# Two graph-attention layers on one core: dense products as four 128x32 column tiles, score products as eight 32x64 tiles

## The chip, the core and the metric

The kernel runs on one core of a Trainium2 chip. The core has a tensor engine (TensorE, PE in the profile, with its weight loads as a row of their own, PEld), a vector engine (DVE), a scalar engine (ACT), GpSimd (POOL) and a queue engine (SP) that issues transfers. The metric is device time in microseconds of one execution; several executions of a kernel are timed and the median is taken.

TensorE multiplies a stationary operand, which is loaded first (a weight load), with a moving operand that streams past it. The stationary operand of a matmul is given as `lhsT` (rows are the contraction, columns become output partitions), the moving one as `rhs`. A matmul may use the whole 128x128 array or a tile of it: a shape such as 128x32 in this text is rows by columns of the stationary operand. Where an operand lies decides the tile: rows by the partitions of the inputs, columns by the partitions of the output.

## The reference

32 graphs of 512 nodes with 256 features each, and an integer adjacency matrix per graph. Two attention layers of 8 heads of 32 follow each other, the first with a feed-forward block of 1024 hidden units, each with residuals and layer norms. Everything is float32.

```python
# layer 0, x: (32, 512, 256), adj: (32, 512, 512)
allowed = (adj > 0) | (swapaxes(adj, 1, 2) > 0) | eye
q, k, v = heads(split(x @ Wqkv.T + bqkv))            # 8 heads of 32
s = where(allowed, (q / sqrt(32)) @ k.T, -inf)
h = layernorm(x + concat(softmax(s) @ v) @ Wo.T + bo)
h = layernorm(h + relu(h @ W1.T + b1) @ W2.T + b2)
x = layernorm(x + h)
# layer 1: attention with the mask adj != 0 and weights of its own
x = layernorm(x + attention(x, adj) @ Wo.T + bo)
```

## The kernel before

The work on one graph is cut into small methods of a class `Graph`, each of which issues a few instructions: a burst on TensorE, an activation, a step of a norm, a transfer. The order is written out by hand. `opening` starts the first graphs, `period` is repeated for the graphs in the middle with up to five graphs in flight (`a` to `e`, each in another stage), and `closing` ends the last ones. Each engine runs its instructions in the order in which these three functions issue them. The trace shows about 95 us for one period.

N is 512 nodes (4 blocks of 128), D is 256 features (2 blocks of 128), a block of 128 features holds 4 heads of 32. Activations are kept with features on the partitions for TensorE (`xT`, `qT`, `kT`, `cT`) and with nodes on the partitions for the norms. The bursts on TensorE, by method:

- `transpose` (L303): four 128x128 transpositions by the identity, into one PSUM tile.
- `query_key` (L332): for one block of 128 output features, two matmuls over the 2 input blocks, moving 512 or 256 nodes. ACT adds the bias (L335).
- `value` (L315): 2 blocks of nodes, each two matmuls moving 256 features. ACT copies (L322).
- `scores` (L345): for one half of the heads and one block of 128 keys, four matmuls, one per head: stationary 32 rows (the head's features) by 128 keys, moving 32 x 512 queries, each into a PSUM bank of its own. ACT then takes the exponential of the whole 128x2048 tile (L349), and DVE multiplies with the mask (`masked`, L354).
- `product` (L362): four matmuls, one per head: stationary 128 keys by 32 features, moving 128 x 512 of the exponentials, into 32 output partitions each; over 4 blocks of keys it accumulates. ACT copies the sum (L372).
- `sums` (L402): the same shape with a stationary block of ones, for the denominators, after DVE and transfers have added up the exponentials (`fold`, L381; `pair`, L377).
- `project` (L461): 2 blocks of nodes, each two matmuls moving 256.
- `hidden` (L481): two blocks of hidden units, each two matmuls moving 256 nodes; ACT applies the ReLU (L489).
- `mlp` (L502): one block of nodes, eight matmuls over the hidden blocks moving 256, one accumulation.

PSUM is shared out so: `ps_s` has one buffer of four banks for scores, `ps_a` one bank for `product`, `ps_d` three single banks for everything else. So a score burst waits until the exponential of the one before has been read, and a dense burst until the one that used its bank three before has been read.

In the kernel before, `query_key`, `value`, `project`, `hidden` and `mlp` use a 128x128 stationary block, as `transpose` does. `scores` uses 32x128 tiles, `product` and `sums` 128x32 tiles.

Of the kernel before, what the change touches and what calls it, by code (L numbers as in the profile page):

```python
# [27 lines left out]
def kernel(ctx: ExitStack, tc: tile.TileContext, t: dict, out: bass.AP):  # L28
# [12 lines left out]
    nc = tc.nc  # L41
    x, adj = t["x"], t["adj"]
    B, N, D = x.shape
    P = 128
    NQ = N // P
    ND = D // P
    HD = D // HEADS
    HPC = P // HD
    DFF = t["L0_gnn_W1"].shape[1]
    NF = DFF // P  # L50
# [36 lines left out]
    def column(name, start=0, size=D):  # L87
# [6 lines left out]
    proj = [  # L94
        (
            [wqkv[:, :, i * D : (i + 1) * D] for i in range(3)],
            column("L0_gnn_bqkv", 0),
            column("L0_gnn_bqkv", D),
            column("L0_gnn_bqkv", 2 * D),
        )  # L100
    ]
    wo = [weight("L0_gnn_Wo")]
    bo = [spread("L0_gnn_bo")]
    w1, b1 = weight("L0_gnn_W1"), column("L0_gnn_b1", 0, DFF)
    w2, b2 = weight("L0_gnn_W2"), spread("L0_gnn_b2")
# [44 lines left out]
    def plain(pools: ExitStack):  # L150
# [8 lines left out]
        def value_bias(layer):  # L159
# [6 lines left out]
            nc.vector.tensor_tensor(bov[layer], ps, bo[layer], ALU.add)  # L166

        def add_row(dst, row):
            nc.gpsimd.dma_start(out=dst, in_=row[:, None, :].to_broadcast([P, NQ, D]), accum_op=ALU.add)
# [7 lines left out]
        class Graph:  # L177
# [129 lines left out]

            def value(self, layer, h):
                if h == 0 and layer != 0:
                    self.tile("v", [NQ, D])  # L310
                ps = ps_d.tile([P, 2, D], F32, tag="d", name=f"psV_{self.b}_{h}")
                for j in range(2):
                    at = slice((2 * h + j) * P, (2 * h + j + 1) * P)
                    for i in range(ND):
                        nc.tensor.matmul(  # L315
                            ps[:, j, :],
                            self.xT[:, i, at],
                            proj[layer][0][2][:, i, :],
                            start=(i == 0),
                            stop=(i == ND - 1),  # L320
                        )
                nc.scalar.copy(self.v[:, 2 * h : 2 * h + 2, :], ps)  # L322

            def query_key(self, layer, which, c, h=None):

                tag = ("qT", "kT")[which]
                dst = getattr(self, tag) if c or h or (which and layer == 0) else self.tile(tag, [ND, N])
                w, bias = proj[layer][0][which], proj[layer][1 + which]
                at = slice(0, N) if h is None else slice(h * 2 * P, (h + 1) * 2 * P)
                ps = ps_d.tile([P, at.stop - at.start], F32, tag="d", name=f"psQK_{self.b}_{which}_{c}_{h}")  # L330
                for i in range(ND):
                    nc.tensor.matmul(  # L332
                        ps, w[:, i, c * P : (c + 1) * P], self.xT[:, i, at], start=(i == 0), stop=(i == ND - 1)
                    )
                nc.scalar.activation(dst[:, c, at], ps, AF.Identity, bias=bias[:, c : c + 1])  # L335


            def scores(self, layer, k):
                if k == 0:
                    self.layer, self.p, self.acc = layer, {}, {}  # L340
                hg, kc = divmod(k, NQ)
                s = ps_s.tile([P, HPC, N], F32, tag="s", name=f"psS_{self.b}_{k}")
                for j in range(HPC):
                    at = slice(j * HD, (j + 1) * HD)
                    nc.tensor.matmul(  # L345
                        s[:, j, :], self.kT[at, hg, kc * P : (kc + 1) * P], self.qT[at, hg, :], start=True, stop=True
                    )
                p = work.tile([P, HPC, N], F32, tag="p", name=f"p_{self.b}_{k}", bufs=8)
                nc.scalar.activation(p, s, AF.Exp, scale=SCALE)  # L349
                self.p[k] = p  # L350
# [101 lines left out]

            def project(self, layer, h):

                if h == 0:
                    self.y, self.po = {}, {}
                ps = ps_d.tile([P, 2, D], F32, tag="d", name=f"psO_{self.b}_{layer}_{h}")
                for j in range(2):
                    at = slice((2 * h + j) * P, (2 * h + j + 1) * P)
                    for k in range(ND):  # L460
                        nc.tensor.matmul(  # L461
                            ps[:, j, :], self.cT[:, k, at], wo[layer][:, k, :], start=(k == 0), stop=(k == ND - 1)
                        )
                self.po[h] = ps
# [6 lines left out]

            def hidden(self, h, f):

                if f == 0:
                    self.hT = getattr(self, "hT", {})
                    self.hT[h] = work.tile([P, NF, 2 * P], F32, tag="hT", name=f"hT_{self.b}_{h}", bufs=1)
                ps = ps_d.tile([P, 2, 2 * P], F32, tag="d", name=f"psH_{self.b}_{h}_{f}")
                for j in range(2):
                    at = slice((f + j) * P, (f + j + 1) * P)
                    for c in range(ND):  # L480
                        nc.tensor.matmul(  # L481
                            ps[:, j, :],
                            w1[:, c, at],
                            self.xT[:, c, h * 2 * P : (h + 1) * 2 * P],
                            start=(c == 0),
                            stop=(c == ND - 1),
                        )
                for j in range(2):
                    nc.scalar.activation(self.hT[h][:, f + j, :], ps[:, j, :], AF.Relu, bias=b1[:, f + j : f + j + 1])  # L489
# [7 lines left out]

            def mlp(self, i):
                h, j = divmod(i, 2)
                ps = ps_d.tile([P, D], F32, tag="d", name=f"psF_{self.b}_{i}")  # L500
                for f in range(NF):
                    nc.tensor.matmul(  # L502
                        ps, self.hT[h][:, f, j * P : (j + 1) * P], w2[:, f, :], start=(f == 0), stop=(f == NF - 1)
                    )
                self.pf[i] = ps
# [36 lines left out]
        def period(a, b, c, d, e):  # L542
# [36 lines left out]
            a.out1(0)  # L579
            a.project(1, 1)  # L580
            b.norm2(2)
# [10 lines left out]
            b.transpose(b.x2, 1)  # L592
            b.query_key(1, 1, 0, 0)
            c.product(4)
# [66 lines left out]
            a.store()  # L661
            d.value(0, 0)
            b.scores(1, 6)
# [16 lines left out]
            c.transpose(c.x1, 1)  # L680
            d.query_key(0, 1, 0)
            d.value(0, 1)
            d.query_key(0, 0, 0)
            d.query_key(0, 0, 1)
            c.mlp(0)
            d.query_key(0, 1, 1)
            c.residual1()
            c.mlp(1)
            b.product(3)
# [18 lines left out]
        def opening(a, b, c, d):  # L708
# [8 lines left out]
            a.join(0, 1)  # L717
            a.query_key(0, 0, 0)
            a.query_key(0, 1, 0)
            a.value(0, 0)  # L720

# [67 lines left out]
            b.scores(0, 3)  # L789
            b.query_key(0, 0, 1)  # L790
            a.project(0, 1)
            b.entries()
# [28 lines left out]
            a.transpose(a.x1, 1)  # L821
            a.mlp(0)
            a.mlp(1)
            a.residual1()
# [25 lines left out]
            a.transpose(a.x2, 0)  # L850
            a.mlp(3)
            a.out2(3)
            b.masked(0, 6)
            a.root(2, 3, 4)
            a.mlp(2)
            a.out2(2)
# [24 lines left out]
            c.join(0, 0)  # L881
            a.query_key(1, 0, 0, 0)
            a.query_key(1, 0, 0, 1)
            a.query_key(1, 1, 0, 1)
            c.value(0, 0)

# [38 lines left out]
            b.transpose(b.x1, 0)  # L925
            c.query_key(0, 1, 0)
            c.masks()
# [15 lines left out]
            b.transpose(b.x1, 1)  # L943
            b.mlp(0)
            b.mlp(1)
            b.residual1()
# [16 lines left out]
        def closing(a, b, c):  # L963
# [8 lines left out]
            c.scores(0, 1)  # L972
            b.hidden(1, 6)
            b.transpose(b.x2, 0)
# [42 lines left out]
            b.transpose(b.x2, 1)  # L1017
            b.query_key(1, 0, 0, 0)
            b.query_key(1, 1, 0, 0)
            c.pair(4)  # L1020
            b.query_key(1, 0, 0, 1)
            c.masked(0, 7)
# [4 lines left out]
            c.fold(3, 3, 4)  # L1027
            b.query_key(1, 1, 1)

# [29 lines left out]
            c.norm1(0)  # L1059
            c.project(0, 1)  # L1060
            c.transpose(c.x1, 0)
# [12 lines left out]
            c.transpose(c.x1, 1)  # L1074
            c.mlp(1)
            c.mlp(0)
            b.masked(1, 6)
# [5 lines left out]
            c.out2(1)  # L1083
            c.hidden(1, 0)
            b.masked(1, 2)
# [3 lines left out]
            c.norm2(1)  # L1089
            c.hidden(1, 4)  # L1090
            c.hidden(1, 6)
            c.hidden(1, 2)
            b.product(0)
# [30 lines left out]
            b.fold(3, 6, 7)  # L1124
            c.query_key(1, 1, 0, 0)
            c.query_key(1, 0, 0, 1)
            c.query_key(1, 1, 0, 1)

# [288 lines left out]
```

## Time and profile before

| | |
|---|---|
| median of 3 runs | 3074.48 us (3072.88 to 3076.89) |
| span of the profiled execution | 3072.4 us |
| DVE busy, mean of one mask or fold (128x2048) | 2648.1 us, 2.28 us |
| ACT busy, one exponential (128x2048) | 1707.3 us, 1.88 us |
| POOL busy | 1039.0 us |
| share of the DMA engines by queue | 51.2% + 16.1% + 0.3% + 0.1% |
| HBM traffic | 40 GB/s over the span |

TensorE's groups, which the profile adds up by line:

| line | burst | instructions | busy us | mean ns |
|---|---|---|---|---|
| L345 | scores | 4096 | 583.9 | 640 |
| L362 | product | 4096 | 492.7 | 598 |
| L502 | mlp | 2048 | 468.5 | 382 |
| L481 | hidden | 2048 | 467.3 | 384 |
| L461 | project | 1024 | 241.0 | 383 |
| L402 | sums | 1072 | 139.8 | 598 |
| L303 | transpose | 520 | 87.3 | 289 |

A matmul's duration in the trace runs from its start to a modelled end and overlaps the next one's, so the mean of one is longer than the time it takes up in a stream; the busy time of a group is the time covered by at least one of its instructions. Each float32 matmul of the program appears as two matmul instructions and two weight loads; a transposition as one of each.

### The profile page before, as it was taken

What the parts mean: (1) busy time and instruction counts of PE and PEld (TensorE: products, weight loads), DVE (VectorE), ACT (ScalarE), POOL (GpSimd) and SP (SyncE); (2) the same over time, 40 slices, a digit from 0 to 9 for tenths busy, and PEclk for the clock granted to TensorE, in tenths of its full rate; (3) what the DMA queues carried; (4) which work ended last, traced back from release to release, by engine and by line L of the source; (5) the groups of instructions that cost most, each with busy time, mean ns of one, the idle gap of its engine ahead of it and who ended that gap; (6) DMA issues with size and microseconds to landing.
All of it is one profiled execution on the core that took longest, in us unless ns stands there. A gap on an engine that the chain in (4) does not pass through costs nothing. (4 is left out here: it accounts for less than half of the span.)

```text
span 3072.4 us, 44237 instructions
## 1 busy us (share of the span) xinstructions
PE 3049.0 (99%) x17218; PEld 1728.9 (56%) x17218; DVE 2648.1 (86%) x3458; ACT 1707.3 (56%) x1983; POOL 1039.0 (34%) x1254
## 2 busy tenths in 40 slices
PE   8999999999999999999999999999999999999998
PEld 4555655556555555555555555655556555555564
DVE  6798889888889888898888988889888889888887
ACT  5455565555556555565556655565555556555554
POOL 1333333433334332343323333333433334332332
PEclk9999999999999999999999999999999999999999
DMA  9876677666767666676666766667766767666543
GB/s 207 155 141 129 116 141 145 140 123 126 136 138 148 121 131 124 138 154 122 133 124 136 148 134 131 114 141 145 139 124 126 136 137 148 120 131 124 117 83 70
DMA packets 341064, 406.54 MB, mean 132 GB/s; under 512 B 149616, under 2 KB 315632, under 8 KB 316144
## 3 DMA queue, kind: packets, MB, share of 16 engines
q0 software_dynamic: 95824, 282.09, 51.2%
q1 hardware_dynamic: 245024, 121.56, 16.1%
q8 instruction: 137, 2.24, 0.3%
q14 instruction: 79, 0.65, 0.1%
HBM read 89.01 MB, written 33.55 MB: 40 GB/s over the span
## 5 line engine op out<-in xcount | busy, mean ns | idle before, releaser
L349 ACT ACTIVATE p<-psS 128x2048 f32<-128x2048 f32 x512 | 962.2, 1879 | 657.1 <-PE psS L345 655.4
L354 DVE TENSOR_TENSOR p<-p,m 128x2048 f32<-128x2048 f32 x512 | 1155.4, 2279 | 8.4 <-ACT p L349 8.2
L436 POOL TENSOR_SCALAR rs<-mv 128x2 f32<-128x2 f32 (+1 forms) x320 | 326.3, 1020 | 940.6 <-DVE mv L431 939.7
L345 PE MATMUL psS<-qT,kT 32*128 32x512 f32 x4096 | 583.9, 640 | 2.8 <-ACT p L349 1.3
L362 PE MATMUL psA<-p,v 128*32 128x512 f32 x4096 | 492.7, 598 | 0.9 <-ACT cT L372 0.7
L502 PE MATMUL psF<-w_L_gnn_W,hT 128*128 128x256 f32 x2048 | 468.5, 382 | 0.0
L481 PE MATMUL psH<-xT,w_L_gnn_W 128*128 128x256 f32 x2048 | 467.3, 384 | 0.7 <-DMA w_L_gnn_W<-in_L_gnn_W_dram 0.7
L502 PEld LDWEIGHTS psF<-w_L_gnn_W,hT 128*128 128x128 f32 x2048 | 383.8, 190 | 123.0 <-issue 76.4
L481 PEld LDWEIGHTS psH<-xT,w_L_gnn_W 128*128 128x128 f32 x2048 | 381.4, 190 | 120.3 <-issue 47.9
L381 DVE TENSOR_TENSOR p<-p,p 128x2048 f32<-128x2048 f32 x189 | 429.5, 2286 | 6.4 <-DMA p<-p 4.7
L345 PEld LDWEIGHTS psS<-qT,kT 32*128 32x128 f32 x4096 | 159.9, 182 | 300.5 <-issue 117.2
L437 POOL TENSOR_TENSOR rs<-rs,neg_half 128x2 f32<-128x2 f32 (+1 forms) x320 | 299.6, 936 | 26.8
L362 PEld LDWEIGHTS psA<-p,v 128*32 128x32 f32 x4096 | 109.9, 109 | 315.3 <-issue 234.5
L489 ACT ACTIVATE hT<-psH,c_L_gnn_b 128x256 f32<-128x256 f32 x512 | 215.2, 472 | 120.6 <-PE psH L481 117.3
L417 POOL TENSOR_TENSOR total<-total,sT 128x16 f32<-128x16 f32 x128 | 28.4, 222 | 732.0 <-DVE sT L414 732.0
L461 PE MATMUL psO<-w_L_gnn_Wo,cT 128*128 128x256 f32 x1024 | 241.0, 383 | 0.9 <-DVE cT L421 0.9
L332 PE MATMUL psQK_None<-xT,w_L_gnn_Wqkv 128*128 128x512 f32 x512 | 238.4, 598 | 2.4 <-DMA w_L_gnn_Wqkv<-in_L_gnn_Wqkv_dram 2.4
L372 ACT COPY cT<-psA 128x512 f32<-128x512 f32 x128 | 75.0, 586 | 280.7 <-PE psA L362 280.7
L377 POOL DMA_DIRECT2D p<-p x189 | 188.2, 996 | 117.8 <-PE psA L362 108.7
L449 DVE TENSOR_TENSOR y<-psF,x 128x256 f32<-128x256 f32 x128 | 53.9, 421 | 200.1 <-PE psF L502 197.6
L461 PEld LDWEIGHTS psO<-w_L_gnn_Wo,cT 128*128 128x128 f32 x1024 | 189.3, 190 | 52.0 <-DVE cT L421 23.0
L430 DVE BATCH_NORM_STATS2 st<-y 128x6 f32<-128x256 f32 x384 | 164.3, 428 | 13.1
(68 smaller groups left out, 2930.8 us busy)
## 6 DMA issues: line engine op xcount, KB each, us to landing
p<-p POOLq DMA_DIRECT2D x189, 1024.0 KB, 7.7
x<-in_x_dram SPq DMA_DIRECT2D x64, 512.0 KB, 5.1
x<-bov POOLq DMA_DIRECT2D x64, 512.0 KB, 9.2
code<-in_adj_dram POOLq DMA_DIRECT2D x32, 512.0 KB, 6.6
m<-code SPq DMA_DIRECT2D x32, 512.0 KB, 5.6
x<-s_L_gnn_ln_b POOLq DMA_DIRECT2D x32, 512.0 KB, 10.4
x<-s_L_gnn_b POOLq DMA_DIRECT2D x32, 512.0 KB, 5.4
out_dram<-x SPq DMA_DIRECT2D x32, 512.0 KB, 9.1
```

The costliest lines, as they stand in the source:

```text
L332: nc.tensor.matmul(ps, w[:, i, c * P : (c + 1) * P], self.xT[:, i, at], start=(i == 0), stop=(i == ND - 1))
L345: nc.tensor.matmul(s[:, j, :], self.kT[at, hg, kc * P : (kc + 1) * P], self.qT[at, hg, :], start=True, stop=True)
L349: nc.scalar.activation(p, s, AF.Exp, scale=SCALE)
L354: nc.vector.tensor_tensor(p, p, m[:, k % NQ, None, :].to_broadcast([P, HPC, N]), ALU.mult)
L362: nc.tensor.matmul(self.acc[hg][j * HD : (j + 1) * HD, :], self.v[:, kc, h * HD : (h + 1) * HD], self.p[k][:, j, :], start=(kc == 0), stop ...
L381: nc.vector.tensor_tensor(self.p[dst], self.p[a], self.p[b], ALU.add)
L436: nc.gpsimd.tensor_scalar(rs, self.mv[n][:, a:b, 1:2], EPS, None, ALU.add)
L437: nc.gpsimd.tensor_tensor(rs, rs, neg_half[:, a:b, None], ALU.pow)
L461: nc.tensor.matmul(ps[:, j, :], self.cT[:, k, at], wo[layer][:, k, :], start=(k == 0), stop=(k == ND - 1))
L481: nc.tensor.matmul(ps[:, j, :], w1[:, c, at], self.xT[:, c, h * 2 * P : (h + 1) * 2 * P], start=(c == 0), stop=(c == ND - 1),)
L489: nc.scalar.activation(self.hT[h][:, f + j, :], ps[:, j, :], AF.Relu, bias=b1[:, f + j : f + j + 1])
L502: nc.tensor.matmul(ps, self.hT[h][:, f, j * P : (j + 1) * P], w2[:, f, :], start=(f == 0), stop=(f == NF - 1))
```

## The change

A new helper `dense` issues one product either as one 128x128 matmul (`wide`) or as four matmuls over 32 columns of the stationary operand each, into 32 output partitions each, with the same moving operand. The five dense methods call it and take an argument `wide`, which is false unless a call in `opening`, `period` or `closing` sets it. It is set at 10 calls of `period` and at further calls of the other two functions, next to `transpose` in the order. `value_bias` and `transpose` stay as they are. `scores` issues two matmuls per head instead of one, for 64 keys each. The order of all bursts and the work of all other engines stay as they were.

```diff
+        def dense(out, lhsT, rhs, start, stop, wide):
+            for at in (slice(0, P),) if wide else [slice(j * HD, (j + 1) * HD) for j in range(HPC)]:
+                nc.tensor.matmul(out[at], lhsT[:, at], rhs, start=start, stop=stop)
...
-            def value(self, layer, h):
+            def value(self, layer, h, wide=False):
...
                     for i in range(ND):
-                        nc.tensor.matmul(
-                            ps[:, j, :],
-                            self.xT[:, i, at],
-                            proj[layer][0][2][:, i, :],
-                            start=(i == 0),
-                            stop=(i == ND - 1),
-                        )
+                        dense(ps[:, j, :], self.xT[:, i, at], proj[layer][0][2][:, i, :], i == 0, i == ND - 1, wide)
...
             def scores(self, layer, k):
...
                     at = slice(j * HD, (j + 1) * HD)
-                    nc.tensor.matmul(
-                        s[:, j, :], self.kT[at, hg, kc * P : (kc + 1) * P], self.qT[at, hg, :], start=True, stop=True
-                    )
+                    for half in range(2):
+                        key = kc * P + half * P // 2
+                        nc.tensor.matmul(
+                            s[half * P // 2 : (half + 1) * P // 2, j, :],
+                            self.kT[at, hg, key : key + P // 2],
+                            self.qT[at, hg, :],
+                            start=True,
+                            stop=True,
+                        )
...
         def period(a, b, c, d, e):
...
-            a.project(1, 1)
+            a.project(1, 1, wide=True)
...
-            b.query_key(1, 1, 0, 0)
+            b.query_key(1, 1, 0, 0, wide=True)
...
-            d.value(0, 0)
+            d.value(0, 0, wide=True)
...
-            d.query_key(0, 1, 0)
-            d.value(0, 1)
-            d.query_key(0, 0, 0)
-            d.query_key(0, 0, 1)
-            c.mlp(0)
-            d.query_key(0, 1, 1)
+            d.query_key(0, 1, 0, wide=True)
+            d.value(0, 1, wide=True)
+            d.query_key(0, 0, 0, wide=True)
+            d.query_key(0, 0, 1, wide=True)
+            c.mlp(0, wide=True)
+            d.query_key(0, 1, 1, wide=True)
             c.residual1()
-            c.mlp(1)
+            c.mlp(1, wide=True)
```

`query_key`, `project`, `hidden` and `mlp` change as `value` does.

## The prediction

> **What bounds the kernel now.** I read the page's busy shares first, then the waits of TensorE (PE), then PE's timeline over some 30 us of a middle period, then the weight loads (PEld).
>
> ```profile
> PE 3049.0 (99%) x17218; PEld 1728.9 (56%) x17218; DVE 2648.1 (86%) x3458; ACT 1707.3 (56%) x1983; POOL 1039.0 (34%) x1254
> ...
> PEclk9999999999999999999999999999999999999999
> ```
>
> ```profile
> PE psT L303 <- DMA x<-in_x_dram: 4.7, 1, 4.7
> PE psQK_None L332 <- DMA w_L_gnn_Wqkv<-in_L_gnn_Wqkv_dram: 2.4, 1, 2.4
> PE psS L345 <- ACT p L349: 1.3, 1, 1.3
> ```
>
> PE is never idle after the opening: 7.1 us of waits there, about 5 us in all the rest, and the full clock throughout. The chain that ended last is only the tail behind the last matmul, so the span is PE's own sequence of bursts. What counts is the time from the start of one burst to the start of the next; a burst's printed length is modelled and overlaps its successor.
>
> ```profile
> 1502.99 1.14 PE L345 MATMUL psS<-qT,kT 32*128 32x512 f32 x8
> 1504.06 3.72 PE L502 MATMUL psF<-w_L_gnn_W,hT 128*128 128x256 f32 x16
> 1507.71 1.06 PE L402 MATMUL psR<-p,ones 128*32 128x512 f32 x8
> 1508.60 1.04 PE L362 MATMUL psA<-p,v 128*32 128x512 f32 x8
> 1509.57 1.14 PE L345 MATMUL psS<-qT,kT 32*128 32x512 f32 x8
> 1510.64 1.07 PE L362 MATMUL psA<-p,v 128*32 128x512 f32 x8
> 1511.63 3.72 PE L502 MATMUL psF<-w_L_gnn_W,hT 128*128 128x256 f32 x16
> ...
> 1520.40 1.14 PE L345 MATMUL psS<-qT,kT 32*128 32x512 f32 x8
> 1521.47 2.78 PE L362 MATMUL psA<-p,v 128*32 128x512 f32 x24
> 1524.18 1.14 PE L345 MATMUL psS<-qT,kT 32*128 32x512 f32 x8
> ...
> 1529.74 1.03 PE L332 MATMUL psQK<-xT,w_L_gnn_Wk 128*128 128x256 f32 x4
> 1530.60 1.03 PE L332 MATMUL psQK<-xT,w_L_gnn_Wq 128*128 128x256 f32 x4
> ```
>
> Columns: start in us, length, engine, line, then stationary shape (rows*columns) and moving shape. Every fp32 product is two instructions (two passes). Three things are to be seen.
>
> First, the streaming price. Four instructions of 256 columns take 0.86 us (1529.74 to 1530.60): 0.215 each, and the single records of such a burst are 0.216 apart. In the 24-instruction product run, four column tiles run side by side: 2.71 us against 0.99 for 8 instructions, so 1.72 us for four more rounds of four, 0.430 a round of 512 columns. A wide 512-column instruction is 0.429 after its predecessor. So four 128x32 tiles together stream as fast as one 128x128 tile; nothing is gained or lost there.
>
> Second, a change of tile shape costs time. Scores take 1.07 us (1502.99 to 1504.06) for 2 rounds, 0.853 at the pure rate: 0.217 lost. A product alone takes 0.99 (1510.64 to 1511.63): 0.137 lost. A wide run of 16 takes 3.65 (1504.06 to 1507.71) against 16 x 0.216 = 3.45: 0.20 lost. Between sums and product (1507.71 to 1508.60), same shape, 0.89: nearly nothing lost.
>
> Third, what the loss is made of:
>
> ```profile
> L345 PEld LDWEIGHTS psS<-qT,kT 32*128 32x128 f32 x4096 | 159.9, 182 | 300.5 <-issue 117.2
> L362 PEld LDWEIGHTS psA<-p,v 128*32 128x32 f32 x4096 | 109.9, 109 | 315.3 <-issue 234.5
> L502 PEld LDWEIGHTS psF<-w_L_gnn_W,hT 128*128 128x128 f32 x2048 | 383.8, 190 | 123.0 <-issue 76.4
> ...
> 1508.17 0.13 PEld L362 LDWEIGHTS psA<-p,v 128*32 128x32 f32 x4 [0.30 <-issue]
> ```
>
> A load of 128 columns takes 190 ns, of 32 columns 109: 0.84 ns a column, so 107 ns against 27 for the columns themselves. Four loads cover 0.13 us at 0.109 each: tiles start 7 ns apart, 20 ns for four. After the last matmul's stream ends, the next shape's first load comes 91 to 95 ns later in the records (the array empties). So wide 94 + 107 = 0.20, product 94 + 27 + 20 = 0.14, scores 91 + 107 + 20 = 0.218: all three measured losses.
>
> **The change, part by part.** I counted runs of one tile shape in the order of PE's instructions. Before: 512 score runs, 420 wide, 260 column; 1191 changes of shape. After, with bursts in the same order: 512, 131, 450; 1092 changes.
>
> Check of the sum: 512 x 0.217 + 420 x 0.20 + 260 x 0.137 = 230.7 us lost to changes. Streaming: 6664 wide passes of 256 x 0.216, 768 of 512 x 0.429, 520 transpositions x 0.109, 1024 score rounds x 0.427, 1292 column rounds x 0.429 = 2817. Together 3048 of the span of 3072.4; the opening (first matmul at 4.7, the weight's wait, slower first matmuls) and the tail behind the last projection hold the rest. The profiled execution lies 2 us below the median of the runs, 3074.5, so I take savings from the median.
>
> Dense products narrow (L163's stays wide): 289 wide runs fewer x 0.20 = -57.8; 190 column runs more x 0.137 = +26.0. Net -31.8 us. The 4964 wide passes that become rounds of four keep 0.216 or 0.429 each.
>
> Scores as 32x64: no row shows this shape. By the load's columns it saves 64 x 0.84 = 54 ns; with eight tiles 7 ns apart the last starts 47 ns behind the first, not 20: +27. Net -27 ns x 512 = -13.8 us. Bounds: as cheap as the product's 0.137, -41 us; load no shorter and the eight starts paid, +27 ns, +13.8 us. I take -13.8, since load and spacing both follow the rows.
>
> PE's instructions grow from 34,436 to 72,412, all loads and matmuls. A narrow round of 256 columns needs eight in 216 ns, 27 ns each. The longest sustained pace shown is lower, 16 in 0.43 us, but one place shows what PE's sequencer can do: while scores waited at 73.45 us, two semaphore instructions ran at 73.29 (51 ns) and 73.415, with the eight instructions of a transposition passed between, 74 ns: 9 ns each. Hidden, then, while the array streams. Their fetch queue (137 packets, 2.24 MB) about doubles; at 256 instructions a packet, one must come every 6.9 us inside a narrow run, against 18.8 at the closest now; a packet takes about 1 us.
>
> The Trainium skill speaks against this part: "TensorE: Matmul & The Clock Gate", section "Wait — 56ns, not 53.3ns?", says that without hardware decode the sequencer spends about 62 ns per matmul, which binds when the array work per matmul is shorter. Narrow rounds of 256 have 54 ns per matmul; by that rule 4 x 62 = 248 ns a round, 32 more in 4680 rounds, an estimated +150 us. The 9 ns of the trace contradict it.
>
> Waits: 187 more of PE's waits are on PE itself, each for a burst at least 1.7 us of matmul time back; queued behind them are only PE's own next bursts, so nothing. ACT, DVE, POOL and SP keep their instructions and order. PE comes earlier by 1.4 us in each period of 95.0 us. Scores wait for the exp of the burst before (one psS buffer): exp at 1518.22 takes 1.88, the next scores start at 1520.40, 0.30 spare; between those two bursts all stays wide, so only 0.027 goes. The tightest repeated wait is the row sums' on DVE's fold, 0.2 us spare in 27 periods. PE gains some 0.35 us over the bursts that feed that fold, so about 0.15 us x 27 = 4 us comes back as waiting. Bounds: none, if DVE moves along (14% idle); (1.4 - 0.2) x 30 = 36 us, if DVE doesn't move at all.
>
> **Sum.** -31.8 - 13.8 + 4 = -41.6 us: 3074.5 - 41.6 = 3033 us.
>
> **The rivals.** *A narrow round isn't free* (slower). Its place is every narrow round of 256 columns: loads of 109 ns, four together 0.13 us, must fit beside 0.213 instead of 0.427 us of stream, and eight instructions must arrive in that time. It decides from 41.6 / 4964 = 8.4 ns a round. If the 28 ns of a load that show at a change of shape showed in every round, 4964 x 0.028 = +139: 3172 us. For it: no row has column tiles with 256 columns. Against: 0.13 fits in 0.213, and wide loads of 190 ns fit there already.
>
> *The gain is eaten by waits*: with the 36 us above and scores without gain, -31.8 + 36 = +4, up to 3078; with half of it, 3060. For it: DVE is 86% busy and mask, fold and norm stand in one fixed order. Against: PE waits hardly ever today, and half the waits that I could place have 1.8 us to spare.
>
> *Score halves don't run side by side* (the tiling doesn't do what it says): both halves of a 32-row strip stream the same qT; if one waits for the other, +0.853 us x 512 = +437, 3470 us. Against: the products' four column tiles stream through the same 128 rows together. The same page of the skill, section "Measured speedup vs the span model", gives 10.6 times for sixteen 32x32 tiles; no run here shows that.
>
> **How the numbers follow.** Forecast 0.80, narrow rounds dear 0.10, eaten 0.06, halves in turn 0.04. The forecast's own range: -31.8 - 41 = -73 (3002) to -31.8 + 13.8 + 11 (a third of the 36) = -7 (3067). Most of the eaten case lies above; dear rounds and serial halves are left out. Under 0.2% (6 us) a measurement of this kernel can't tell from no change. Faster 0.82 (the forecast and a little of the eaten case), same 0.04, slower 0.14 (both dear cases).
>
> **What would show it.** PE stays near 99%. Scores start to next start 1.04 us (1.07 before); 0.98 or 1.10 would be the bounds. A narrow mlp of 32 matmuls (x64) 16 x 0.216 plus at most 0.14. No gap between narrow hidden and product. PE's waits for DVE grow by about 4 us. It is wrong if rounds of four start over 0.224 us apart, if score records of one strip start 0.43 us apart, or if PE waits add 20 us or more.

## The result and the profile after

| | before | after |
|---|---|---|
| median of the timed runs, taken side by side | 3074.28 us (3072.88 to 3078.45, 12 runs) | 3074.61 us (3071.69 to 3078.51, 12 runs) |
| ratio, 95% interval | 1 | 1.0001 (0.9993 to 1.0009) |
| span of the profiled execution | 3072.4 us | 3073.1 us |
| one period in the middle, median from start to start | 94.79 us | 94.68 us |

The change moves nothing that can be measured; the forecast was 3033 us. The period is read from the trace's records, as the distance between the first score bursts of successive graphs.

The page of the changed kernel, its busy shares and the chain that ended last, by engine:

```profile
PE 3019.5 (98%) x36206; PEld 1393.8 (45%) x36206; DVE 2648.4 (86%) x3458; ACT 1702.8 (55%) x1983; POOL 1044.9 (34%) x1254
...
DVE 49%; PE 35%; issue 8%; DMA 4%; POOL 4%; ACT 0%; SPq 0%; DVEq 0%; POOLq 0%; ACTq 0%
```

PE is busy 29.5 us less than before in a span that is as long. And the chain, which was only the tail behind the last matmul, now runs through the whole span, half of it on DVE. PE's waits after (engine, tile and line, what it waited for; us in total, times, longest):

```profile
PE psT L308 <- DVE x L448: 21.2, 34, 0.7
PE psR L405 <- DVE p L384: 6.1, 6, 2.4
...
PE psS L344 <- ACT p L352: 2.1, 9, 0.6
```

The first of these was 0.9 us, 2 times, before, and the second wasn't in the list. The first is the transposition of x1, which needs the first norm's output from DVE. Busy times of PE in the first half of the steady stretch (from and to, length, PE busy with its instructions, PEld, DVE, ACT, POOL, clock, DMA share, GB/s), before and then after:

```profile
260.00:1530.00 1270.00, 1269.85 (x7194) 721.47 (x7187) 1111.39 (x1455) 713.03 (x827) 445.79 (x530) 1.00 0.69 134
```

```profile
260.00:1530.00 1270.00, 1257.75 (x15240) 579.27 (x15236) 1111.21 (x1456) 710.08 (x826) 451.01 (x530) 1.00 0.69 134
```

DVE does the same work in the same stretch; PE's idle time went from 0.15 to 12.25 us.

The prices of the bursts themselves came out as forecast. PE's timeline after:

```profile
1504.28 1.11 PE L344 MATMUL psS<-qT,kT 32*64 32x512 f32 x16
1505.32 3.66 PE L171 MATMUL psF<-w_L_gnn_W,hT 128*32 128x256 f32 x64
...
1512.89 3.64 PE L171 MATMUL psF<-w_L_gnn_W,hT 128*32 128x256 f32 x64
1516.34 1.91 PE L171 MATMUL psO<-w_L_gnn_Wo,cT 128*32 128x256 f32 x32
```

Scores take 1.04 us from start to start (1.07 before), and a narrow mlp of 64 instructions ahead of a burst of the same shape 3.45 us, 16 rounds of 0.216.

Now the place of the wait. Before, PE and then DVE:

```profile
1556.20 0.66 PE L303 MATMUL psT<-ident,x 128*128 128x128 f32 x4
1556.69 1.89 PE L315 MATMUL psV<-w_L_gnn_Wqkv,xT 128*128 128x256 f32 x8
```

```profile
1555.77 0.48 DVE L445 SCALAR_TENSOR_TENSOR x<-cent,rs,s_L_gnn_ln_b 128x256 f32<-128x256 f32 x1
```

After, PE and then DVE:

```profile
1556.81 0.33 PE L308 MATMUL psT<-ident,x 128*128 128x128 f32 x1
1557.85 0.55 PE L308 MATMUL psT<-ident,x 128*128 128x128 f32 x3 [0.71 <-DVE x L448]
```

```profile
1557.31 0.48 DVE L448 SCALAR_TENSOR_TENSOR x<-cent,rs,s_L_gnn_ln_b 128x256 f32<-128x256 f32 x1
```

The burst transposes two blocks of x1. Its first instruction needs the first block, the second one the second block, whose norm is this DVE instruction. After, the second starts 1.04 us behind the first instead of 0.11: PE stands 0.93 us **inside** the burst. Before, the burst already started at 1556.20, ahead of the end of that norm at 1555.77 + 0.48 = 1556.25; the second load starts at 1556.31 in the records. So the norm came just in time, with nothing to spare. In most of the kernel's other transpositions, which nothing holds up, the second load starts 0.056 to 0.061 us behind the first, here 0.113: PE already waited for the norm by some 0.05 us, and no wait was listed.

Why doesn't DVE move along? All of its gaps between 1535 and 1600 us before, and the first three of them after (in brackets the gap and what ended it):

```profile
1554.73 0.48 DVE L445 SCALAR_TENSOR_TENSOR x<-cent,rs,s_L_gnn_ln_b 128x256 f32<-128x256 f32 x1 [0.92 <-POOL rs L437]
1578.79 0.42 DVE L449 TENSOR_TENSOR y<-psF,x 128x256 f32<-128x256 f32 x1 [2.40 <-PE psF L502]
1583.96 0.42 DVE L449 TENSOR_TENSOR y<-psF,x 128x256 f32<-128x256 f32 x1 [4.07 <-PE psF L502]
1586.34 0.48 DVE L445 SCALAR_TENSOR_TENSOR z<-cent,rs,x 128x256 f32<-128x256 f32 x1 [0.91 <-POOL rs L437]
1590.21 0.73 DVE L518 TENSOR_SCALAR x<-z,mv,rs 128x256 f32<-128x256 f32 x2 [1.13 <-POOL rs L437]
```

```profile
1556.27 0.48 DVE L448 SCALAR_TENSOR_TENSOR x<-cent,rs,s_L_gnn_ln_b 128x256 f32<-128x256 f32 x1 [0.92 <-POOL rs L440]
1580.22 0.42 DVE L452 TENSOR_TENSOR y<-psF,x 128x256 f32<-128x256 f32 x1 [2.28 <-PE psF L171]
1585.39 0.42 DVE L452 TENSOR_TENSOR y<-psF,x 128x256 f32<-128x256 f32 x1 [4.07 <-PE psF L171]
```

DVE's idle 14%, some 13 us a period, isn't slack that can be spent anywhere. Half of it is two waits for the mlp products (`out2`), 2.40 and 4.07 us, which end 22 and 28 us after the transposition; the other gaps are latencies of about 1 us inside DVE's own norms, where POOL works out `rs`. From the second `y` of one period to the norm of the next, DVE's work is a chain with nothing but such latencies in it. It starts with these lines, before and after, one period ahead of those shown above:

```profile
1489.17 0.42 DVE L449 TENSOR_TENSOR y<-psF,x 128x256 f32<-128x256 f32 x1 [4.07 <-PE psF L502]
```

```profile
1490.63 0.42 DVE L452 TENSOR_TENSOR y<-psF,x 128x256 f32<-128x256 f32 x1 [4.07 <-PE psF L171]
```

It ends with the norm at 1556.25 and 1557.79: 67.1 and 67.2 us. Then PE goes from the second transposition to the end of the second mlp product: 27.65 us before (1556.31 to 1583.96), 27.54 after (1557.85 to 1585.39). With some 0.05 us from the norm's end to the load that it releases, this **loop through both engines** takes 94.79 us before and 94.76 after, the length of just these periods (most of those after have 94.67). Any path from one event to the same event of the next period adds up to that; what makes this one a bound is that no step of it has time to spare. The chain that ended last shows it after (start, length, what):

```profile
1548.49 4.48 DVE p L357 x2
1555.52 0.73 POOL rs L440
1556.27 0.49 DVE x L448
1556.79 0.50 DVE cent L447
1557.31 0.50 DVE x L448
1557.85 0.55 PE psT L308 x3
1558.40 1.73 PE psV L171 x8
...
1581.89 3.45 PE psF L171 x16
```

Before, PE's own sequence took 94.78 us, the period of the two runs below that relieve the loop in that kernel (`e4_before_mlp_early`, `e6_before_no_mask`): two bounds within some 0.01 us of each other. The change shortened one of them by 1.4 us. In the other, it touches two score bursts (2 x 0.027) and one run of `hidden` between scores (0.20 - 0.137): 0.12 us.

### The profile page after: what moved, and what is told of

Same layout as the page of the kernel before. It is cut to its first block, busy times and chain, and to the rows that moved or that the text cites. A ratio compares the mean times of both kernels' runs of the same rounds, so it can differ in the third digit from the quotient of the medians.

```text
span 3073.1 us, 82394 instructions
## 1 busy us (share of the span) xinstructions
PE 3019.5 (98%) x36206; PEld 1393.8 (45%) x36206; DVE 2648.4 (86%) x3458; ACT 1702.8 (55%) x1983; POOL 1044.9 (34%) x1254
## 4 chain that ended last, share of the span: by engine, by line
DVE 49%; PE 35%; issue 8%; DMA 4%; POOL 4%; ACT 0%; SPq 0%; DVEq 0%; POOLq 0%; ACTq 0%
DVE p L357 18%; PE psH L171 8%; PE psF L171 8%; DVE p L384 8%; PE psQK_None L171 7%; DVE st L433 5%; PE psS L344 3%; PE psV L171 3%; DVE y L452 3%; DVE rT L423 3%; DVE sT L417 2%; DMA p<-p 2%; POOL rs L440 2%; DVE cT L424 2%; DVE mv L434 2%
## 5 line engine op out<-in xcount | busy, mean ns | idle before, releaser
L439 POOL TENSOR_SCALAR rs<-mv 128x2 f32<-128x2 f32 (+1 forms) x320 | 294.6, 921 | 943.5 <-DVE mv L434 941.7
L344 PE MATMUL psS<-qT,kT 32*64 32x512 f32 x8192 | 571.1, 613 | 2.9 <-ACT p L352 2.1
L171 PE MATMUL psF<-w_L_gnn_W,hT 128*32 128x256 f32 (+1 forms) x5024 | 464.1, 380 | 0.0
L171 PE MATMUL psH<-xT,w_L_gnn_W 128*32 128x256 f32 x8072 | 461.7, 380 | 0.5 <-DMA w_L_gnn_W<-in_L_gnn_W_dram 0.5
L171 PEld LDWEIGHTS psF<-w_L_gnn_W,hT 128*32 128x32 f32 (+1 forms) x5024 | 326.1, 127 | 169.6 <-issue 70.8
L171 PEld LDWEIGHTS psH<-xT,w_L_gnn_W 128*32 128x32 f32 x8072 | 260.1, 110 | 233.0 <-issue 49.9
L344 PEld LDWEIGHTS psS<-qT,kT 32*64 32x64 f32 x8192 | 119.3, 130 | 319.4 <-issue 133.5
L171 PE MATMUL psO<-w_L_gnn_Wo,cT 128*32 128x256 f32 (+1 forms) x3352 | 240.1, 380 | 1.4 <-DVE cT L424 1.4
L171 PE MATMUL psQK_None<-xT,w_L_gnn_Wqkv 128*128 128x512 f32 (+1 forms) x608 | 238.6, 598 | 2.4 <-DMA w_L_gnn_Wqkv<-in_L_gnn_Wqkv_dram 2.4
L171 PEld LDWEIGHTS psO<-w_L_gnn_Wo,cT 128*32 128x32 f32 (+1 forms) x3352 | 141.5, 116 | 97.5 <-DVE rT L423 23.5
```

The source lines that it names most:

```text
L171: nc.tensor.matmul(out[at], lhsT[:, at], rhs, start=start, stop=stop)
L344: nc.tensor.matmul(s[half * P // 2 : (half + 1) * P // 2, j, :], self.kT[at, hg, key : key + P // 2], self.qT[at, hg, :], start=True, stop ...
L439: nc.gpsimd.tensor_scalar(rs, self.mv[n][:, a:b, 1:2], EPS, None, ALU.add)
```

## The experiments

The theory after the result: the loop sets the period at 94.67 us, while PE's own sequence fell to 94.79 - 1.41 = 93.38 us. The rival: PE didn't get faster by what was forecast, and its wait is only a by-product. Ratios below are against the kernel before, timed beside each run.

**One half of the change each.** `e1_scores_only` is the kernel before with 32x64 score tiles, `e2_dense_only` the changed kernel with 32x128 ones.

```diff
 e2_dense_only, against after
-                    for half in range(2):
-                        key = kc * P + half * P // 2
-                        nc.tensor.matmul(s[half * P // 2 : (half + 1) * P // 2, j, :], ...)
+                    nc.tensor.matmul(
+                        s[:, j, :], self.kT[at, hg, kc * P : (kc + 1) * P], self.qT[at, hg, :], start=True, stop=True
+                    )
```

> The kernel before with only the score products as eight 32x64 tiles; dense products stay 128x128. Theory (the period is set by a loop that leaves DVE at its norm for c.transpose, runs through PE from there to c.mlp(1), and comes back through DVE; PE's work outside that stretch has room and is worth nothing): two of a period's 16 score bursts lie in the stretch, 2 x 0.027 us x 30 periods = 1.6 us, so 3072.9, no change that can be measured. Rival (PE's own sequence sets the period, as the prediction had it): 512 x 0.027 = 13.8 us, so 3060.7.

> The changed kernel with score products back as four 32x128 tiles; dense products stay in column tiles. Theory (loop through DVE and one stretch of PE): the changed kernel plus 1.6 us, 3076, and TensorE's waits for DVE in a period fall from 1.4 to about 1.0 us. Rival (PE's own sequence): dense products alone save 289 x 0.20 - 190 x 0.137 = 31.8 us, 3043.

Measured: 3079.43 us for the scores, ratio 1.001 (1.0001 to 1.0019), and 3073.56 us for the dense products, 0.9996 (0.9987 to 1.0005). The periods are 94.74 and 94.75 us. By the loop they should be 94.79 - 0.054 and 94.79 - 0.063: each half brings its own few hundredths and nothing of the rest, though the dense half alone takes 31.8 us over 32 graphs, 1.0 us from PE's sequence in each period, by the forecast's prices. The first run's time misses the theory by 6.5 us; its opening is 8.4 us longer in the profile (first steady scores, those of the second call of `period`, at 269.0 us, 260.6 before), with waits of 3.6 us for ACT's `xT`, 2.3 for DVE's fold and 1.9 for an exponential. All 11 runs are at 3077 us or above, so it isn't one uneven execution. But openings differ by themselves too: in the runs below that leave the code of `opening` as in the changed kernel, these scores start anywhere from 260.6 to 267.2 us. Whether the score tiles cause the longer one was not tried by itself and stays open.

**The loop cut on PE's side.** The two wide mlp products end the loop. In `period` they go ahead of three other bursts that DVE doesn't wait for; everything else stays.

```diff
             d.query_key(0, 1, 0, wide=True)
+            c.mlp(0, wide=True)
+            c.mlp(1, wide=True)
             d.value(0, 1, wide=True)
             d.query_key(0, 0, 0, wide=True)
             d.query_key(0, 0, 1, wide=True)
-            c.mlp(0, wide=True)
             d.query_key(0, 1, 1, wide=True)
             c.residual1()
-            c.mlp(1, wide=True)
```

`e3_after_mlp_early` does this to the changed kernel, `e4_before_mlp_early` to the one before.

> The changed kernel; in the repeated period c.mlp(0) and c.mlp(1) stand right after the first query_key of graph d, and d's value and other three query_key products after them. Work and results are the same. Theory: DVE waits 2.4 and 4.1 us in each period for these two products; they come 5.2 and 6.9 us earlier, so the loop through DVE gets some 6 us shorter and PE's own sequence, 94.79 - 1.41 = 93.38 us, sets the period: 1.3 us x 28 periods = 36 us less, about 3038, and TensorE's wait at the transposition of x1 is gone. Rival (column tiles cost as much as they save somewhere in PE): no change, 3074.

> The kernel before with the same move of c.mlp(0) and c.mlp(1). Theory: there PE's own sequence is as long as the loop through DVE (94.78 us), so a shorter loop brings nothing: 3074, within 3 us. Rival (the loop through DVE alone set the period of the kernel before, and PE had room): up to 1 us in each period, 3045.

Measured: 3057.2 us, ratio 0.9939 (0.9926 to 0.9953), and 3074.62 us, ratio 1.0 (0.9991 to 1.0009). The same move is worth 18 us in the changed kernel and nothing in the one before, as the theory says; but only half of what it expected, with a period of 94.08 us. The reason, PE and then DVE in the first of these:

```profile
1547.09 0.33 PE L308 MATMUL psT<-ident,x 128*128 128x128 f32 x1
1547.92 0.55 PE L308 MATMUL psT<-ident,x 128*128 128x128 f32 x3 [0.50 <-DVE x L448]
```

```profile
1522.29 2.29 DVE L357 TENSOR_TENSOR p<-p,m 128x2048 f32<-128x2048 f32 x1 [0.62 <-ACT p L352]
```

The transposition still waits. Its burst takes 0.67 us longer than an unhindered one, which is nearly the distance of the period from PE's own sequence (94.08 - 93.40, worked out below). DVE's long gaps at `y` are gone, and a shorter loop seems to have come up behind the first: DVE's mask waits 0.62 us for an exponential, so for PE's scores, some 25 us ahead of the norm.

**DVE's side of the loop.** `e5_after_no_mask` and `e6_before_no_mask` leave out one mask multiply of the period, 2.28 us of DVE ahead of that norm, from the changed kernel and from the one before; one block of the second layer stays unmasked.

```diff
-            b.masked(1, 1)
             b.scores(1, 5)
```

> The changed kernel with one mask multiply of the period left out (b.masked(1, 1), 2.28 us of DVE in each of the steady periods; the output then lacks that block's mask in the later layer). Theory: DVE runs back to back for some 67 us of each period up to the norm that the transposition of x1 waits for, and this stretch plus PE's 27.5 us behind it sets the period at 94.69 us; with 2.28 us less on DVE, PE's own sequence of 93.38 us is the bound, 1.3 us x 27 periods = 35 us less: 3039 us, and the transposition's stall of 1.05 us in the middle goes to nothing. Rival (PE lost its gain elsewhere, so that DVE does not matter): 3074 us. A loop through DVE that binds beside it, as in the run with the mlp products early: 3055 us.

> The kernel before with the same mask multiply left out. Theory: there PE's own sequence of 94.78 us sets the period and DVE's stretch only just equals it, so 3074 us, no change. Rival (DVE set the end already in the kernel before): 3074 - 27 x 2.28 = 3013 us at most, and anything below 3065 us speaks for it.

Measured: 3044.7 us, ratio 0.9906 (0.9891 to 0.9921), and 3072.03 us, ratio 0.9992 (0.9983 to 1.0001). This is the sharpest of the tests: the same 2.28 us off DVE are worth 30 us in one kernel and 2 in the other, whose period stays 94.78 us. In the changed kernel without the mask, the chain, the transposition, and DVE's gap at `y`:

```profile
PE 91%; DVE 5%; DMA 2%; POOL 1%; ACT 1%; issue 0%; SPq 0%; POOLq 0%; DVEq 0%
```

```profile
1541.01 1.11 PE L344 MATMUL psS<-qT,kT 32*64 32x512 f32 x16
1542.06 0.66 PE L308 MATMUL psT<-ident,x 128*128 128x128 f32 x4
```

```profile
1564.53 0.42 DVE L452 TENSOR_TENSOR y<-psF,x 128x256 f32<-128x256 f32 x1 [3.42 <-PE psF L171]
```

The burst is whole again, x4, and PE is the chain. DVE's gap at `y` grew from 2.28 to 3.42 us: now DVE waits for PE. The period is 93.73 us; a wait of 0.33 us is left in it, row sums on DVE's fold. 93.73 - 0.33 = 93.40 is PE's own sequence, against the expected 93.38. That wait, 28 x 0.33 = 9 us, is why the time lies above the expected 3039 us.

**An order that computes everything.** The mask isn't left out but goes behind the norm, and its product (`product(1)`) behind the transposition: `e8_after_mask_late`; with the two mlp products early as well: `e7_after_both`.

```diff
-            b.masked(1, 1)
             b.scores(1, 5)
...
             c.norm1(1)
+            b.masked(1, 1)
             b.product(0)
-            b.product(1)
             b.product(2)
...
             c.hidden(0, 0)
+            b.product(1)
             b.pair(0)
```

> The changed kernel with the second of these moves alone (b.masked(1, 1) behind c.norm1(1), b.product(1) behind c.hidden(0, 0)). Theory: DVE's stretch to the norm is 2.28 us shorter, and PE reaches the y that starts the next stretch 0.86 us later for the product moved behind the transposition: 1.42 us off the loop, which is more than the 1.31 us between it and PE's own sequence: 3039 us. Rival (the loop runs through the mlp products' end and is cut by moving these alone): 3074 us.

> The changed kernel, everything computed, with two moves in the period: c.mlp(0) and c.mlp(1) right after d.query_key(0, 1, 0), as in the run that gave 3057 us, and b.masked(1, 1) behind c.norm1(1) on DVE, with b.product(1) behind c.hidden(0, 0) on PE. Theory: 2.28 us of DVE and 0.86 us of PE leave the stretch ahead of the transposition of x1, so that its wait of 0.5 to 0.8 us goes too and PE's own sequence of 93.38 us sets the period: 3038 us. Rival (what is left of the wait in the run with 3057 us is not DVE's order but a fixed latency): 3057 us.

Measured: 3054.55 us, ratio 0.9936 (0.9923 to 0.995), period 93.99; and **3046.4 us, ratio 0.9903 (0.9888 to 0.9918)**, period 93.66, which beats both kernels. The waits at the transposition are gone in both runs. What is left: in the first 0.31 us at the row sums and 0.26 at the scores that now come earlier (93.40 + 0.57 = 93.97), 16 us in 28 periods and so the distance from the expected 3039; in the second only the latter, its chain and this line:

```profile
PE 91%; DVE 3%; DMA 2%; ACT 2%; POOL 0%; issue 0%; SPq 0%; POOLq 0%; DVEq 0%
```

```profile
1544.75 1.12 PE L344 MATMUL psS<-qT,kT 32*64 32x512 f32 x16 [0.18 <-ACT p L352]
```

93.66 - 0.26 = 93.40 us: the same own sequence of PE by a second way. The time is 8 us above the expected 3038: 7 us are this wait; the opening of the profiled execution was longer too (267.2 us to the first steady scores, 262.6 after).

**Is it the order alone?** For the last four runs the transposing loads, of the mask's code and of the input, are plain loads of the same number of bytes (the input's from the adjacency), which also asks whether they take part.

```diff
-                    nc.sync.dma_start_transpose(out=self.m1[:, i, :], in_=self.code[:, i * P : (i + 1) * P])
+                    nc.sync.dma_start(out=self.m1[:, i, :], in_=self.code[:, i * P : (i + 1) * P])
...
-                    src = x[self.b, i * 2 * P : (i + 1) * 2 * P, :]
-                    nc.sync.dma_start_transpose(out=self.flipped(0, i), in_=src.bitcast(U16))
+                    src = adj[self.b, i * P : (i + 1) * P, :].bitcast(U16)
+                    nc.sync.dma_start(out=self.flipped(0, i), in_=src.rearrange("p (a q) -> p a q", q=2 * P))
```

The base and the changed kernel:

> The kernel before with its transposing loads (the mask's code and each graph's input) replaced by plain loads of the same number of bytes, the input's from the adjacency: the masks are not transposed and the first layer's products take other numbers, everything else is issued in the same order. It is the base of the three runs beside it. Theory: no transfer is in the loop that sets the steady period, so the period stays PE's own, 94.78 us; the opening may shorten by some us: 3068 to 3074 us. If a period differs by over 0.1 us, the loads take part in it.

> The changed kernel with the same plain loads. Theory: the loop of DVE's 67 us and PE's 27.5 us sets the period as before this replacement, 94.67 us, with PE waiting about 0.93 us inside the transposition of x1: within 4 us of the run of the kernel before with plain loads. Rival (transposing loads took part in the wait): a period of 93.4 us and 35 us less.

Measured: 3072.77 us (3072.17 to 3073.71), period 94.80, and 3069.35 us (3068.11 to 3070.8), period 94.67, the transposition's wait 0.93 us again. So the loads take no part in the steady state. And here a small gain can be seen in the time: 28 periods x 0.13 = 3.6 us, measured 3.4. That the two agree is partly luck: in the profiled executions a few uneven periods take 1.6 us back, and 1.1 us are won behind the periods. With the transposing loads a longer opening hid it (262.6 us to the first steady scores against 260.6; 260.3 and 260.4 here).

The kernel before in the order of the 3046 us, and the changed kernel with a third move against the 0.26 us:

```diff
             c.project(0, 0)
-            c.project(0, 1)
+            b.product(0)
             b.scores(1, 3)
+            c.project(0, 1)
```

> The kernel before with plain loads and with both moves of the run that gave 3046 us (the two mlp products early; one mask multiply behind the norm, its product behind the transposition). Theory: PE's own sequence sets the period there, so the order around the norm is worth nothing: period 94.78 us, the time of the kernel before with plain loads within 3 us. Rival (the new order by itself gave the 28 us, the column tiles have no part in it): 28 us less than that.

> The changed kernel with plain loads, both moves, and a third: b.product(0) between c.project(0, 0) and b.scores(1, 3), and c.project(0, 1) behind that, so that b.scores(1, 7), which waited 0.26 us in each period for ACT's exponential, comes no earlier than ACT has ended. Theory: nothing but PE's own sequence is left, 93.66 - 0.26 = 93.40 us a period; 27 x (94.78 - 93.40) = 37 us less than the kernel before with plain loads, and PE shows no wait in the steady periods. Rival (ACT or DVE takes over at once): a period of 93.66 us or more, 30 us less at most.

Measured: 3086.47 us (3085.5 to 3087.29), period 95.33, and 3049.41 us (3048.62 to 3050.92), period 93.91. Both expectations on the theory's side missed. The order alone makes the kernel before 14 us **slower** than its base. Its PE timeline shows where:

```profile
1564.46 1.99 PE L477 MATMUL psH<-xT,w_L_gnn_W 128*128 128x256 f32 x8
1566.38 1.07 PE L358 MATMUL psA<-p,v 128*32 128x512 f32 x8
1567.38 2.86 PE L477 MATMUL psH<-xT,w_L_gnn_W 128*128 128x256 f32 x12
```

There `hidden` is wide, so the moved product breaks a wide run: one more column run and one more wide one, 0.137 + 0.20 = 0.34 us by the forecast's prices, and the product moved away from ahead of scores makes them wait 0.21 us for the exponential, as in the run of 3046 us; 0.53 measured in the period. In the changed kernel `hidden` has the product's shape and the move is free. So the order of the 3046 us is no gain by itself: with the old tiles its period is 95.33 us, with the new ones 93.66 (with transposing loads, which moved no steady period above by more than 0.02 us). The third move was the wrong one: the product now waits 0.35 us in the shortest periods and up to 1.0 in the longest, by the profile for an exponential of ACT or its mask on DVE, and the rival, 30 us at most, was right with 23.

## Why the prediction was wrong

**The streaming price and the changes of shape were right.** Rounds start 0.216 us apart, scores take 1.04, and PE's own sequence fell by 94.79 - 93.40 = 1.39 us a period where the working had 1.4. The 8.4 ns a round from which the first rival decides did not appear, and the halves of the scores run side by side.

**The step that failed is the waits.** "The tightest repeated wait is the row sums' on DVE's fold, 0.2 us spare in 27 periods", and from it "about 0.15 us x 27 = 4 us comes back as waiting". The wait of the sums was found rightly, at half its size (0.31 us now). But the tightest was another, with zero spare: the second instruction of the transposition on the norm of x1. The working weighs the waits ahead of bursts; this one sits inside a burst. In place of 0.15 us, 1.28 us of 1.39 came back in each period: 0.93 at the transposition, 0.31 at the sums, and some hundredths elsewhere. So the term of +4 us should have been some +36 (28 x 1.28). Over the profiled execution, 28 periods x 0.11 us and 1.3 us behind them are won, 2.0 us are lost in the opening and 3 in a few uneven periods: nothing is left. One of the signs that the text names for being wrong came with it, 20 us or more of added waits: those listed grew by 20 us at the transposition and by 6 at the sums.

**"None, if DVE moves along (14% idle)" was the wrong reading of the share.** DVE could not move along: its idle time lies in waits that end with PE's own mlp products, 27.5 us behind the transposition, and from there to the next norm its work has no gap but its own latencies. The upper bound in the same place, 36 us "if DVE doesn't move at all", met the size, in part by luck: it sets off 0.2 us a period that the sums had to spare, where the runs show 0.11 that the change takes off the loop.

**The rival that held** is "the gain is eaten by waits", and its sentence "mask, fold and norm stand in one fixed order" names the mechanism. Its end at 3078 us rests on scores without a gain; but the scores did gain (1.07 to 1.04 us). It had 0.06 because of "PE waits hardly ever today". That argument proves nothing in a kernel where two bounds are equal: an engine that never waits shows that its suppliers are on time, not by how much.

**The page's rule.** The estimate of +150 us from the 62 ns per matmul of the Trainium skill, "TensorE: Matmul & The Clock Gate", "Wait — 56ns, not 53.3ns?", did not come: 64 narrow instructions take 3.45 us, 54 ns each, the price of the wide ones (16 x 0.216 us). The page gives the 62 ns for hardware decode off; no run here shows whether it is on. The working's own pace before the change, "16 in 0.43 us", should read 8 where it is sustained: a round of products has four loads and four matmuls.

## What to carry to other kernels

An engine at 99% can be one of two bounds. Before you price a gain on it, follow each engine that feeds it for one whole period, list the gaps of that engine and what ends them, and add up every loop that runs through both; the smallest difference between those loops and the bound, with what the change takes off that loop itself, is all that it can bring. Look at the waits inside a burst too, not only at its start, and at instructions that start just as their input ends. And when a change brings nothing, test the other bound on both kernels: relief that helps only the changed one shows where the gain went.

## What the runs showed of the hardware

Column tiles run side by side in rounds: in the records of the changed kernel four narrow matmuls start 7 ns apart (1513.102, .109, .116, .122) and the next four 0.216 us after the first, with loads of 110 ns beside them; eight instructions, loads and matmuls, for each round, sustained over 64 matmuls.

A few periods are longer than the rest by 1 to 1.5 us, and at the same places in different kernels: counted from the first steady scores, the 5th, 15th and 24th after (95.85, 96.20 and 96.21 us) and with its tiles in most other orders, the 16th in the kernel before (95.80). In the 15th one after, DVE's fold waits 1.49 us for the accumulating transfer of the exponentials. They cost 3 us more after than before; why just there stays open.
